# One run for the seven output products, 64x64 scan-input products in two banks, and new dates in the planner of an attention kernel

## The chip, the core and the metric

The kernel runs on one core of a Trainium2 chip. The metric is the device time of one execution in microseconds (us); the time of before is the median of three executions. The profile comes from one further execution. Engine names are those of the profile: PE is TensorE (matmuls), PEld its weight loads, DVE is VectorE, ACT is ScalarE, POOL is GpSimd, SP the queue that issues most DMAs.

## The reference, cut to what matters

One sequence of 4096 rows by 512, a context of 3202 rows, 8 heads of 64, all float32. Layer norm of both, multi-head cross attention with output weights `W_o`, residual; then a layer norm, a projection to 64 scan inputs, a scan over all 4096 rows, its states times `Cmat` added, and a constant row.

```python
x = residual + _mha(layernorm(x), layernorm(ctx), W_qkv, b_qkv, W_o, b_o)
residual = x
U = (layernorm(x) @ W_in.T + b_in) @ Bmat           # 4096 x 64
def step(s, u_t):
    s = jax.nn.silu(s @ A.T) + u_t
    return (s, s)
_, states = jax.lax.scan(step, zeros, U)
x = residual + states @ Cmat + mod
```

## The kernel before, in words

**Lead.** For the first 195 us keys and values are computed from the context and stored in DRAM. **Attention.** The 4096 query rows are eight blocks of 512 (`Q` 0 to 7). A block has 8 units (4 pairs of heads by 2 halves of 256 rows), and a unit has 13 steps over the keys. A step is a batch of scores (L1133, tile `s`, two PSUM buffers), an exponential on ACT (L1211, tile `p`, a ring of 11), a running sum of the exponentials on DVE (L1219, tile `acc`) and a batch of products with the values (L1269, tile `po`), four steps later. Scores and value products use the PE array as four 64x64 quarters: four matmuls run at once, one on each quarter. A full step is 8 matmuls of each kind, which the trace holds as 16 records, two for each float32 matmul. Two quarters that read different rows write to different PSUM banks. The sums over keys (`sums`, L1298, tile `pd`) and the first guess of the maximum (`sample`, `spread`, L1153 and L1175, tile `sm`) are also in quarters.

**Between the steps** stands the rest of a block, and it repeats from block to block. The query projection of the next block (`by_sevenths`) and the output projection of the last one (`project_by_sevenths`) are products of two 2x2 block matrices, done with seven block products instead of eight, with the whole 128x128 array (`seventh`, L393, 8 records for each of the seven). They accumulate in two PSUM banks, x and y, in the order 1, 2, 6, 5, 7, 3, 4 (`CHAIN`). After each product its bank is read (`read`), and the next product into the same bank waits for that read, so there is a chain PE, reader, PE with one other product between. The readers are ACT and DVE in turn for the queries, and DVE alone for the outputs (L1667, `outs.read`). Four sums of operands (`sum_`, L1649, pieces `so`) are made on DVE for products 5, 6, 7 and 3. In the output projection, sum 5 is made only after product 1 (`open_left` is called by product 1, and the plan says so), product 5 waits for it, and so the seven products are broken into three runs with scores between. In the query projection the sums are made ahead, and its seven products are one run.

After the output projection each half block of 256 rows goes through a second layer norm, is transposed (DVE `flip`, then DMAs `move0` to `move3` on SP into tile `xn2`), and is multiplied with the 512x64 matrix `wc` to give the scan inputs (`inputs`, L1729, tile `pu`): for each of 4 chunks and 2 row tiles one matmul of 128 rows by 64 columns, 16 records, all into one PSUM bank. ACT reads the bank with two activations (`kept_rows`, L1758) into the tile `u`.

**Ring m.** `sample`, `sums`, the seven products and `inputs` share two PSUM banks, the ring `m`; whoever takes them waits until the reader of the one before has given them back.

**Order.** All pieces of the attention part go through `Plan`: a piece has an engine, a cost, the pieces it needs, a due time, rings that it takes, and a `kind`. `order` walks through time and gives each free engine the ready piece that is due first. A due time is shifted for each sort of piece by the table `SHIFT` (in steps of 2150 ns). On PE, pieces of kind `"quarters"` and pieces without a kind are told apart: changing over costs `ENTER` or `LEAVE` in the plan, and a piece that would stand alone in the other mode is put off by `ALONE`. The order that comes out is the program's order on each engine; nothing is reordered on the chip between engines' queues. Scores, value products, `sums`, `sample` and `spread` are quarters; `inputs` and the seven products are not.

**Tail.** The last block has only its first half projected in this way (`project`); the last 256 rows follow at the end (`last_rows`): output product L2076, layer norm, transposes (L334, L2115), their scan inputs (L2125), and a short scan of 20 dependent steps (tile `zl` and, for the last four, `py_o`, L1924 with ACT L2161). Beside it runs the main scan's second sweep, 16 dependent steps (tile `z`, L1924, ACT L1952, DVE L1959), and the rows of the output (L1998, then ACT, POOL, DVE and a store).

Of the kernel before, what the change touches and what calls it, by code (L numbers as in the profile page):

```python
# [75 lines left out]
class Plan:  # L76
# [11 lines left out]
    KEEP, ALONE = 6000, 30000  # L88
# [5 lines left out]
        "row.store": -0.5, "fold": 17, "rows.outs": 10.5, "heads": -12, "spread": 1.75, "query.flip": -11,  # L94
        "states": -17, "inverse": 14.75, "extra": 10, "scale": -55.75, "rest": 11, "row.mod": -20,
        "joined0": -6.25, "b": -1, "add.l": -23, "l.stats": -34.25, "last": -4.5, "base": -34.75,
        "inverse.l": -35, "rows.inputs": 6, "maximum": -13.75, "fall": -19, "query.stats": -4, "den": 6.5,
        "row.scaled": 16, "l.h": -11, "row.stats": -21.25, "rows.turn": 13, "query.scaled": 7.5, "l.mod": 7.5,
        "close": -10, "swap": -2.25, "products": -9, "gather.l": -4, "l.ys": -10, "fall.l": -2.5,
        "weights": -3.5, "rows.s": 2, "l.x1": 1, "l.kept": 6, "tq": 20, "l.store": 10, "row.move3": 11,  # L100
        "l.from": -5, "l.copy": -12, "l.states": -8, "l.turn": 4, "row.flip": 3.75, "swap.l": -18, "l.near": 4,
        "differ": 12.25, "row.load": 12, "add": -6, "rest.l": -8, "den.l": 11.5, "query.factors": 16,
        "sevenths": -6, "l.z": 1, "scale.l": -0.5, "outs": -3, "output": -12, "query.move3": 3, "number": 0.25,
        "l.inputs": -4, "q": -12, "sums": -4, "row.move2": 2, "row.move1": -0.25, "query.move0": 1.5,
        "stored1": -12, "counted": 1, "to": 12, "sums.l": 1, "row.kept": 8, "so": 10.75, "stored0": 2,
        "l.scaled": -0.25, "row.move0": 4, "rise": 3, "join": -12, "sample": 3.5, "l.idle": 11.75,
        "risen": -0.5, "c2": 1, "yb": 2, "query.load": 8, "query.move2": -4, "row.row": -0.5, "added": -12,
        "l.terms": 13, "joined1": 2,
# [23 lines left out]
    def order(self):  # L132
# [11 lines left out]
        last, now, port, before, events, out = None, 0, 0, None, [], []  # L144
# [7 lines left out]
        def fits(p):  # L152
            if shares(p) and port + (self.LATE["DVE"] if gated(p) else 0) > now:
                return False
# [7 lines left out]
        while len(out) < len(pieces):  # L162
            for e in self.LATE:
# [22 lines left out]
                for r in p["take"]:  # L186
                    taken[r].append(p["name"])
# [2478 lines left out]
```

## Time and profile before

| | us |
|---|---|
| median of 3 executions | 1901.77 (1901.64 to 1901.78) |
| the profiled execution's own time | 1901.72 |
| its span in the profile | 1899.8 |
| PE busy | 1884.8 (99%) |
| DVE busy | 1545.2 (81%) |
| ACT busy | 1178.1 (62%) |
| POOL busy | 253.5 (13%) |

The profiled execution's own time is 1.9 us more than its span. A matmul's start in the trace is measured and its end is modelled, and matmuls overlap; so the time of a stretch of PE work is read from the start of its first matmul to the start of the first matmul behind it. From 351.4 us to 1594.2 us the trace repeats itself every 207.1 us, six times, once for each block; the seventh projection falls into the stretch behind it. The page's section on the chain that ended last is empty in this profile, so what bounds the kernel is read from stretches and from the order in time.

### The profile page before, as it was taken

What the parts mean: (1) busy time and instruction counts of PE and PEld (TensorE: products, weight loads), DVE (VectorE), ACT (ScalarE), POOL (GpSimd) and SP (SyncE); (2) the same over time, 40 slices, a digit from 0 to 9 for tenths busy, and PEclk for the clock granted to TensorE, in tenths of its full rate; (3) what the DMA queues carried; (4) which work ended last, traced back from release to release, by engine and by line L of the source; (5) the groups of instructions that cost most, each with busy time, mean ns of one, the idle gap of its engine ahead of it and who ended that gap; (6) DMA issues with size and microseconds to landing.
All of it is one profiled execution on the core that took longest, in us unless ns stands there. A gap on an engine that the chain in (4) does not pass through costs nothing.

```text
span 1899.8 us, 68757 instructions
## 1 busy us (share of the span) xinstructions
PE 1884.8 (99%) x29632; PEld 1383.5 (73%) x29632; DVE 1545.2 (81%) x2114; ACT 1178.1 (62%) x1677; POOL 253.5 (13%) x386
## 2 busy tenths in 40 slices
PE   9999999999999999999999999999999999999997
PEld 5887678777777777777777777777777777777684
DVE  6642699788978898799978897889969997988776
ACT  3242677575767567666766576657766675657653
POOL 6120300022000310022002200021002200120105
PEclk9999999999999999999999999999999999999999
DMA  8654233133323343223413332324312331536476
GB/s 254 159 158 118 59 103 91 41 112 91 97 74 105 92 110 89 77 76 105 112 43 113 83 110 78 105 78 113 101 55 89 112 104 44 171 111 177 136 200 225
DMA packets 260768, 207.55 MB, mean 109 GB/s; under 512 B 94632, under 2 KB 233896, under 8 KB 260460
## 3 DMA queue, kind: packets, MB, share of 16 engines
q1 hardware_dynamic: 256440, 196.48, 36.3%
q10 hardware_dynamic: 4020, 6.62, 1.2%
q8 instruction: 235, 3.85, 0.9%
q14 instruction: 73, 0.60, 0.1%
HBM read 156.32 MB, written 29.88 MB: 98 GB/s over the span
## 4 chain that ended last, share of the span: by engine, by line


## 5 line engine op out<-in xcount | busy, mean ns | idle before, releaser
L1211 ACT ACTIVATE p<-s,shifts 128x1024 f32<-128x1024 f32 (+1 forms) x832 | 895.0, 1082 | 458.1 <-PE s L1133 441.4
L1219 DVE TENSOR_TENSOR acc<-p,acc 128x1024 f32<-128x1024 f32 (+1 forms) x704 | 838.1, 1191 | 107.8 <-ACT p L1211 82.9
L1269 PE MATMUL po<-p,v 64*64 64x256 f32 x12800 | 849.5, 377 | 0.9 <-DVE o L1324 0.9
L1133 PE MATMUL s<-q,k 64*64 64x256 f32 x12800 | 850.1, 377 | 0.3 <-ACT p L1211 0.2
L1133 PEld LDWEIGHTS s<-q,k 64*64 64x64 f32 x12800 | 505.0, 133 | 197.2 <-ACT p L1211 12.9
L1269 PEld LDWEIGHTS po<-p,v 64*64 64x64 f32 x12800 | 504.0, 133 | 172.1 <-issue 6.9
L1622 POOL TENSOR_TENSOR xr<-xr,rowb 128x512 f32<-128x512 f32 x28 | 35.4, 1275 | 842.5 <-DVE acc L1219 842.5
L1347 DVE RECIPROCAL rd<-rd 128x256 f32<-128x256 f32 (+1 forms) x64 | 110.1, 1720 | 9.7 <-ACT rd L1342 9.7
L1219 DVE TENSOR_TENSOR acc<-p,p 128x1024 f32<-128x1024 f32 x64 | 78.1, 1220 | 26.5 <-ACT p L1211 26.4
L1713 POOL TENSOR_TENSOR xr<-x,modb 128x512 f32<-128x512 f32 x28 | 35.5, 1277 | 197.5 <-DVE acc L1219 155.5
L1243 DVE TENSOR_TENSOR acc<-swap,acc 64x256 f32<-64x256 f32 x126 | 56.1, 446 | 1.8 <-ACT swap L1238 0.2
L1204 DVE TENSOR_TENSOR acc<-x,acc 2x256 f32<-2x256 f32 x128 | 54.9, 429 | 1.4
L1409 POOL TENSOR_SCALAR rstd_x<-mv_x 128x1 f32<-128x1 f32 x28 | 18.9, 677 | 269.7 <-DVE mv_x L1406 268.0
L1559 ACT ACTIVATE q<-qx,bias 128x256 f32<-128x256 f32 x42 | 17.6, 471 | 56.8 <-PE qx L393 56.8
L1238 ACT COPY swap<-acc 64x256 f32<-64x256 f32 x126 | 50.9, 404 | 3.0
L571 DVE TENSOR_TENSOR ks<-pky,ks 128x512 f32<-128x512 f32 x15 | 10.4, 692 | 42.9 <-PE pky L393 28.1
L565 ACT ACTIVATE ks<-pkx,bias 128x256 f32<-128x256 f32 x40 | 16.8, 471 | 42.7 <-PE pkx L393 31.2
L1226 DVE TENSOR_TENSOR acc<-acc 128x512 f32<-128x512 f32 x63 | 42.9, 682 | 0.4
L1324 DVE TENSOR_TENSOR o<-po,o 128x256 f32<-128x256 f32 x64 | 26.9, 421 | 8.8 <-ACT o L1320 8.7
L1342 ACT ACTIVATE rd<-pd 128x128 f32<-128x128 f32 x126 | 33.6, 276 | 0.1
L1417 ACT ACTIVATE xh_y<-x,nm_y,rstd_y 128x512 f32<-128x512 f32 x30 | 24.3, 808 | 13.1 <-POOL nm_y L1411 13.1
L1167 DVE TENSOR_REDUCE m<-sm 128x1 f32<-128x256 f32 x64 | 23.8, 413 | 10.1 <-PE sm L1153 10.1
(312 smaller groups left out, 1754.2 us busy)
## 6 DMA issues: line engine op xcount, KB each, us to landing
k<-kd SPq DMA_DIRECT2D x432, 128.0 KB, 2.3
v<-vd SPq DMA_DIRECT2D x432, 128.0 KB, 2.3
xn<-x SPq DMA_DIRECT2D x448, 32.0 KB, 1.9
xr<-in_x_dram SPq DMA_DIRECT2D x30, 256.0 KB, 3.8
x1d<-xr SPq DMA_DIRECT2D x30, 256.0 KB, 2.8
x<-in_x_dram SPq DMA_DIRECT2D x28, 256.0 KB, 3.0
cx<-in_ctx_dram SPq DMA_DIRECT2D x25, 256.0 KB, 5.0
kd<-ks SPq DMA_DIRECT2D x20, 256.0 KB, 2.3
```

The costliest lines, as they stand in the source:

```text
L1133: nc.tensor.matmul(s[k0 : k0 + HD, a, b, :], kts[(*w["at"][:2], c)][r, b * CK + k0 : b * CK + k0 + HD], q[r], start=True, stop=True, skip_ ...
L1204: made = nc.vector.tensor_tensor(to[r], t[r], to[r], ALU.add)
L1211: nc.scalar.activation(t[:, :, :nb, :], w["ps"][c][:, :, :nb, :], AF.Exp, bias=w["shift"])
L1219: return nc.vector.tensor_tensor(w["acc"][:, :, :nb, :], t[:, :, :nb, :], before[:, :, :nb, :], ALU.add)
L1226: return nc.vector.tensor_tensor(acc[:, :, 0, :], acc[:, :, 0, :], acc[:, :, 1, :], ALU.add)
L1238: nc.scalar.copy(w["swap"][r], of[(1 - k) * HD : (2 - k) * HD])
L1243: made = nc.vector.tensor_tensor(of[r], w["swap"][r], of[r], ALU.add)
L1269: nc.tensor.matmul(w["po"][k][a * HD : (a + 1) * HD, :QU], vts[Q, hp, c][r, b, a * HD : (a + 1) * HD], t[r, a, b, :], start=(c == 0 and b ...
L1342: nc.scalar.activation(to, of, AF.Copy, accum_out=rises[:, 3 * i + k : 3 * i + k + 1])
L1347: nc.vector.reciprocal(w["rd"][:, part], (w["pd"] if last else w["rd"])[:, part])
L1622: return nc.gpsimd.tensor_tensor(xs[half][:, t], xs[half][:, t], rowb, ALU.add)
L1713: return nc.gpsimd.tensor_tensor(xt[:, t], x1[:, t], modb, ALU.add)
```

## The change

**Output projection.** The four operand sums of the output projection no longer wait for product 1 and product 5's sum no longer follows it; sum 5 opens the operands itself (`open_left` returns at once when they are open). Product 1 now waits for sums 6 and 7. Reads of both projections get a due time earlier by `ALONE`, which puts them ahead of other ready pieces of their engine. A new rule in `fits` keeps an engine from beginning a piece that would hold up an expected read by more than `WAITS` (600 ns).

**Scan inputs.** Each matmul of `inputs` is split by its 128 rows into two of 64, one for each of two banks, and the piece becomes a `"quarters"` piece that takes both banks of ring m: 16 matmuls (32 records) in place of 8 (16 records). ACT moves the first bank, with bias and scale, into the start of `xn2` (`first`, one 128x128 activation in place of two 64x128), and DVE adds the second bank to it and writes `u` (`kept_sums`, two SCALAR_TENSOR_TENSOR of 64x128). The tail's own inputs (L1843 and L2125) stay as they were.

**Dates.** The table `SHIFT` gets other numbers for nearly all sorts and 22 more sorts; the due times of almost all pieces of the attention part move.

```diff
-    KEEP, ALONE = 6000, 30000
+    KEEP, ALONE, WAITS = 6000, 30000, 600
+    CHAINS = "outs", "sevenths"
...
-        "row.store": -0.5, "fold": 17, "rows.outs": 10.5, "heads": -12, "spread": 1.75, "query.flip": -11,
+        "row.store": 2.25, "fold": 21, "rows.outs": -27.25, "heads": 29.5, "spread": 4.5, "query.flip": -21,
...
         def fits(p):
+            if any(now < r < now + p["cost"] - self.WAITS for r in reads.get(p["engine"], [])[-2:]):
+                return False
...
+                    if p["name"][0] in self.CHAINS:
+                        on = pieces[(p["name"][0] + ".read", *p["name"][1:])]["engine"]
+                        reads[on].append(now + cost + self.LATE[e])
...
         def open_left():
+            if left:
+                return
...
             if k == "5":
+                open_left()
...
-            after = {"5": scales(*a21) + scales(*a22) + [(*key, "1")], "6": [("so", Q, "5")],
+            after = {"5": scales(*a21) + scales(*a22), "6": [("so", Q, "5")],
...
-            "1": scales(*a11) + [("to", "4")] + [(*k, "row") for ks in kss for k in ks],
+            "1": scales(*a11) + [("to", "4")] + [("so", Q, k) for k in "67"]
+            + [(*k, "row") for ks in kss for k in ks],
...
-            plan.add(("outs.read", Q, k), "DVE", 690, partial(read, k), [(*key, k)], d + at,
+            plan.add(("outs.read", Q, k), "DVE", 690, partial(read, k), [(*key, k)], d + at - plan.ALONE,
...
-            w["pu"] = m_tile([P, P], f"pu_{at[0]}")
+            w["pu"] = [m_tile([P, P], f"pu_{at[0]}_{k}") for k in range(2)]
...
-                    nc.tensor.matmul(
-                        w["pu"][t * NS : (t + 1) * NS], wc[:, c, :], mixed(w["xn"][:, c, :], t),
-                        start=(c == 0), stop=(c == NC - 1), skip_group_check=True,
-                    )
+                    for k in range(2):
+                        r = slice(k * HD, (k + 1) * HD)
+                        nc.tensor.matmul(
+                            w["pu"][k][t * NS : (t + 1) * NS], wc[r, c, :], mixed(w["xn"][r, c, :], t),
+                            start=(c == 0), stop=(c == NC - 1), skip_group_check=True,
+                        )
...
-        plan.add((*k2, "inputs"), "PE", 850, inputs, copied + [from_(d + (gate + 12) * STEP)],
-                 d + 16 * STEP, ["m"], [("xn2", xn2)])
+        plan.add((*k2, "inputs"), "PE", 900, inputs, copied + [from_(d + (gate + 12) * STEP)],
+                 d + 16 * STEP, ["m", "m"], [], "quarters")
+
+        def first():
+            w["sum"] = w["xn"][:, 0, :P]
+            nc.scalar.activation(w["sum"], w["pu"][0], AF.Identity, bias=bu2, scale=2.0)
...
+    def kept_sums(w, at, t):
...
+        nc.vector.scalar_tensor_tensor(
+            u[hs, :, c0 : c0 + P // L].rearrange("s j c -> s c j"),
+            w["pu"][1][of].rearrange("s (c j) -> s c j", j=L),
+            2.0,
+            w["sum"][of].rearrange("s (c j) -> s c j", j=L),
+            ALU.mult,
+            ALU.add,
+        )
```

What this makes of the order, first on PE at the output projection of block 1. Names: `pax` and `pay` are the banks x and y, `s` scores, `po` value products; in the kernel before, the middle one of the three runs:

```order
L1133 MATMUL s_0_1_11_7775<-q_0_6561,k_0_0_11_7156 64x256 x8
L393 MATMUL pay_7735<-to_2260,so_7756 128x256 x4
L393 MATMUL pax_7734<-to_2260,so_7756 128x256 x4
L393 MATMUL pay_7735<-wo,o_2_0_6209 128x256 x4
L393 MATMUL pax_7734<-to_2316,o_0_1_5181 128x256 x4
L1269 MATMUL po_2_0_1_7585<-p_0_1_7_7664,v_0_0_7_7158 64x256
```

Ahead of this stand products 1 and 2, then a batch of `po` and one of `s`; behind it stand batches of `po`, `s` and `po`, and then product 4 alone. In the changed kernel, the same place on PE:

```order
L1280 MATMUL po_2_0_1_7599<-p_0_1_9_7749,v_0_0_9_7232 64x256
L404 MATMUL pax_7840<-wo,o_0_0_4720 128x256 x4
L404 MATMUL pay_7841<-wo,o_2_0_6211 128x256 x4
L404 MATMUL pax_7840<-to_2277,so_7785 128x256 x4
L404 MATMUL pay_7841<-to_2277,so_7785 128x256 x4
L404 MATMUL pax_7840<-to_2337,o_0_1_5177 128x256 x4
L404 MATMUL pay_7841<-wo,o_2_0_6211 128x256 x4
L404 MATMUL pax_7840<-to_2337,o_2_1_6583 128x256 x4
L1144 MATMUL s_1_0_1_7913<-q_0_6602,k_1_0_1_7561 64x256 x8
```

The seven are one run, and it begins about two steps later in the block than the first of the three runs did; this holds for all seven blocks that have it. On DVE, which reads the banks (L1667 before, L1682 after) and makes the sums (L1649 before, L1664 after), the same place in the kernel before:

```order
L1667 TENSOR_TENSOR x_512_7754<-pax_7734,xr_7182 128x2x256
L1649 TENSOR_TENSOR so_7756<-o_0_1_5181,o_2_1_6567 128x512
L1667 TENSOR_TENSOR x_512_7754<-pay_7735,x_512_7754 128x2x256
L1649 TENSOR_TENSOR so_7756<-so_7756,o_0_0_4721 128x512
L1649 TENSOR_TENSOR o_0_1_5181<-o_0_0_4721,o_0_1_5181 128x512
L1649 TENSOR_TENSOR o_2_0_6209<-o_2_0_6209,so_7756 128x512
L1219 TENSOR_TENSOR acc_0_1_7530<-p_0_1_8_7688,acc_0_1_7530 128x1024
L1667 TENSOR_TENSOR x_768_7798<-pay_7735,xr_7214 128x2x256
```

And on DVE in the changed kernel, from the read of product 1 to that of product 3:

```order
L1682 TENSOR_TENSOR x_512_7857<-pax_7840,xr_7200 128x2x256
L1230 TENSOR_TENSOR acc_0_1_7549<-p_0_1_10_7760,acc_0_1_7549 128x1024
L1682 TENSOR_TENSOR x_512_7857<-pay_7841,x_512_7857 128x2x256
L1664 TENSOR_TENSOR o_2_0_6211<-o_2_0_6211,so_7785 128x512
L1682 TENSOR_TENSOR x_512_7857<-pax_7840,xr_7200 128x2x256
L1230 TENSOR_TENSOR acc_0_1_7549<-p_0_1_11_7792,acc_0_1_7549 128x1024
L1682 TENSOR_TENSOR x_768_7884<-pay_7841,xr_7255 128x2x256
L1230 TENSOR_TENSOR acc_0_1_7549<-p_0_1_12_7812,acc_0_1_7549 128x2x256
L1237 TENSOR_TENSOR acc_0_1_7549<-acc_0_1_7549 128x2x256
L1682 TENSOR_TENSOR x_768_7884<-pax_7840,x_768_7884 128x2x256
L1682 TENSOR_TENSOR x_512_7857<-pay_7841,x_512_7857 128x2x256
```

Three of the four sums now stand ahead of the run, and between two reads stand at most two other pieces. In the tail, on PE behind the last output products, the kernel before has the second transpose, then two scan steps with rows of the output, then the second half's inputs (L2125), and the terms of the short scan (`zl`) behind the seventh step of the main scan:

```order
L1998 MATMUL pd_last<-c_21297,scan 64x256 x8
L1924 MATMUL z<-scan,a_t 64x128 x2
L2125 MATMUL py_o_24447<-xn_l,wc 64x128 x4
L1924 MATMUL z<-scan,a_t 64x128 x2
L1924 MATMUL z<-u,a_t 64x512 x2
...
L1924 MATMUL z<-scan,a_t 64x128 x2
L1924 MATMUL zl<-scan,a_t 64x128 x8
L1924 MATMUL py_o_24447<-scan,a_t 64x128 x2
```

In the changed kernel the inputs of both halves stand together behind the second transpose, and the terms of `zl` follow behind the third step of the main scan:

```order
L2151 MATMUL py_o_24587<-ident,xh_yl_24599 128x128 x4
L2161 MATMUL pu_l_24615<-xn_l,wc 64x128 x4
L2161 MATMUL py_o_24587<-xn_l,wc 64x128 x4
L1960 MATMUL z<-scan,a_t 64x128 x2
...
L1960 MATMUL zl<-scan,a_t 64x128 x8
L1960 MATMUL py_o_24587<-scan,a_t 64x128 x2
L1960 MATMUL z<-scan,a_t 64x128 x2
L2034 MATMUL pd_last<-c_21416,scan 64x256 x4
```

The short scan moved ahead by four steps of the main scan, which now stand behind its start. The lead, up to the first scores, stands on every engine as before.

More of the change, by code (lines that the diff above doesn't have):

```diff
@@ L99 @@
[L99 to L103, printed above, removed]
@@ L143, in order @@
         free = dict.fromkeys(self.LATE, 0)
-        last, now, port, before, events, out = None, 0, 0, None, [], []
+        last, now, port, before, reads, events, out = None, 0, 0, None, dict(DVE=[], ACT=[]), [], []
         def shares(p):
```

38 lines of the change are left out of this document (26 added, 12 removed).

## The prediction, made before the change was run

> **What bounds the kernel now.** I began with the busy shares, then cut the span into stretches, and then read PE's order in time at the places that the change touches.
>
> ```profile
> span 1899.8 us, 68757 instructions
> PE 1884.8 (99%) x29632; PEld 1383.5 (73%) x29632; DVE 1545.2 (81%) x2114; ACT 1178.1 (62%) x1677; POOL 253.5 (13%) x386
> ```
>
> The table by stretches has, behind each span, the busy time of PE, PEld, DVE, ACT and POOL; here are the first and the last of six equal periods, and the end:
>
> ```profile
> 351.40:558.50 207.10, 207.07 (x3541) 150.50 (x3541) 179.07 (x234) 137.24 (x188) 22.61 (x32) 1.00 0.33 91
> ...
> 1387.10:1594.20 207.10, 207.07 (x3544) 150.41 (x3540) 179.23 (x234) 137.39 (x189) 22.62 (x32) 1.00 0.32 91
> ...
> 1850.00:1899.80 49.80, 38.89 (x490) 24.03 (x490) 31.63 (x76) 15.61 (x53) 24.71 (x31) 0.94 0.71 227
> ```
>
> PE is occupied for 207.07 of 207.1 us, at the full clock (1.00), while DVE has 28 us and ACT 70 us free. So PE is the bound, and work moved to DVE is free as long as PE does not wait for it. But "busy" covers drains, so I go to the starts. The output projection of block 1, all of PE's rows:
>
> ```profile
> 635.59 1.24 PE L1269 MATMUL po<-p,v 64*64 64x256 f32 x16
> 636.46 1.24 PE L1133 MATMUL s<-q,k 64*64 64x256 f32 x16
> 637.62 1.99 PE L393 MATMUL pax<-wo,o 128*128 128x256 f32 x8
> 639.45 1.89 PE L393 MATMUL pay<-wo,o 128*128 128x256 f32 x8
> 641.27 1.09 PE L1269 MATMUL po<-p,v 64*64 64x256 f32 x16
> 642.19 1.04 PE L1133 MATMUL s<-q,k 64*64 64x256 f32 x16
> 643.16 1.99 PE L393 MATMUL pay<-to,so 128*128 128x256 f32 x8
> ...
> 648.44 1.89 PE L393 MATMUL pax<-to,o 128*128 128x256 f32 x8
> 650.26 1.09 PE L1269 MATMUL po<-p,v 64*64 64x256 f32 x16
> ...
> 651.61 1.04 PE L1269 MATMUL po<-p,v 64*64 64x256 f32 x16
> 652.58 1.99 PE L393 MATMUL pax<-to,o 128*128 128x256 f32 x8
> 654.51 1.09 PE L1133 MATMUL s<-q,k 64*64 64x256 f32 x16
> ```
>
> A batch of 16 quarter records takes 0.87 us (635.59 to 636.46). Each time PE leaves the quarters it loses more: 636.46 + 0.87 is 637.33 and the first product starts at 637.62 (0.29 lost), 643.06 against 643.16 (0.10), 652.48 against 652.58 (0.10). The runs themselves last 3.65, 7.10 and 1.93 us up to the next quarter matmul, 12.68 together.
>
> **Term 1, one run in place of three.** What one run costs is in the trace, since the query projection has the same seven products with the same shapes:
>
> ```profile
> 752.70 0.61 PE L1269 MATMUL po<-p,v 64*64 64x256 f32 x8
> 753.24 1.99 PE L393 MATMUL qx<-xn,wq 128*128 128x256 f32 x8
> ...
> 763.70 1.89 PE L393 MATMUL qx<-xn,wq 128*128 128x256 f32 x8
> 765.52 1.09 PE L1133 MATMUL s<-q,k 64*64 64x256 f32 x16
> ```
>
> It lasts 12.28 us, with 0.11 at its entry (8 records are 0.43): 12.39. Now the outputs cost 12.68 + 0.29 + 0.10 + 0.10 = 13.17. The difference is 0.78 us a block. Of it 0.19 is the surplus of the first entry (0.29 against 0.10), which no row explains and which may stay; I count **0.59**, and keep 0 to 0.19 more for the range. Seven blocks: 4.1 us.
>
> **Term 2, scan inputs in quarters.** The two places in one block:
>
> ```profile
> 690.94 1.04 PE L1133 MATMUL s<-q,k 64*64 64x256 f32 x16
> 691.92 1.09 PE L1729 MATMUL pu<-xn,wc 128*64 128x128 f32 x16
> 692.94 1.09 PE L1269 MATMUL po<-p,v 64*64 64x256 f32 x16
> ...
> 735.87 1.15 PE L1269 MATMUL po<-p,v 64*64 64x256 f32 x16
> 736.94 1.09 PE L1729 MATMUL pu<-xn,wc 128*64 128x128 f32 x16
> 737.97 1.09 PE L1133 MATMUL s<-q,k 64*64 64x256 f32 x16
> ```
>
> The first costs 0.11 at the entry (690.94 + 0.87 to 691.92) and 1.02 up to the next batch, the second 0.20 and 1.03: 2.36 us a block. The new form, 32 records of 64x64 by 128 columns, does not occur, but `pd` has records of that very shape in the same mode:
>
> ```profile
> 655.42 0.40 PE L1298 MATMUL pd<-acc,ones 64*64 64x128 f32 x8
> 655.64 1.04 PE L1269 MATMUL po<-p,v 64*64 64x256 f32 x16
> ```
>
> 8 records in 0.22 us, so 32 in 0.88 and two places in 1.76. Gain 0.60 us a block, seven blocks: 4.2 us. Its bounds are no loss of mode changes at all (0.60) and, should the doubled count cost as much as the changes saved, 0.
>
> **What DVE and ACT get.** For each half block ACT gives up two activations and takes one, and DVE takes two additions. Prices:
>
> ```profile
> L1758 ACT ACTIVATE u<-pu,bu 64x128 f32<-64x128 f32 x30 | 14.4, 480 | 5.9 <-PE pu L1729 4.9 <-PE pu L1843 0.7
> L1952 ACT ACTIVATE scan<-z 128x128 f32<-128x128 f32 x16 | 4.5, 279 | 14.7 <-PE z L1924 14.7
> L1959 DVE SCALAR_TENSOR_TENSOR scan<-scan,z 128x128 f32<-128x128 f32 x16 | 4.5, 284 | 7.6 <-ACT scan L1952 5.9 <-PE zl L1924 1.6
> ```
>
> ACT: 2 x 0.48 less, 0.28 more, so 1.4 us a block less. DVE: four additions a block at 0.28, or 0.48 if writing `u` with its stride costs DVE what it costs ACT: 1.1 to 1.9 us of the 28 that are free. That hides, on average. What doesn't follow from an average is the place: both banks of ring m are now held until DVE has added, and in the new order `sums` stands three batches behind the first half's inputs, 3 x 0.87 = 2.6 us. From the last input to the freed banks it takes one activation and two additions, 0.28 + 0.56, behind at most one running exponential and one running `acc` (1.1 and 1.2 us, row below). That is 0.8 to 3.2 us, so at worst 0.6 us of waiting; DVE's order has a row statistic and no `acc` just ahead of the additions, so I count nothing.
>
> **The wait that the change makes tight** is the read of each product. Rows of DVE:
>
> ```profile
> 645.26 0.69 DVE L1667 TENSOR_TENSOR x<-pay,xr 128x512 f32<-128x512 f32 x1 [0.18 <-PE pay L393]
> 645.87 1.22 DVE L1219 TENSOR_TENSOR acc<-p,acc 128x1024 f32<-128x1024 f32 x1
> 647.00 0.68 DVE L1667 TENSOR_TENSOR x<-pax,xr 128x512 f32<-128x512 f32 x1
> ```
>
> Product 5 starts at 643.16 and is read from 645.26 on: 2.1 us after its start. A product comes every 1.73 us ((648.44 - 643.16 - 0.10) / 3, the 0.10 being what a run loses behind its first matmul), and the product that needs this read starts 3.46 + 0.10 after it. Left over: 3.56 - 2.10 - 0.69 = 0.77 us. In the new order I followed DVE's queue with these rows (a read holds the next piece up for 0.61 us, an `acc` for 1.13): the reads of products 1, 2, 6, 5 and 7 end at 2.8, 4.5, 6.2, 8.0 and 9.8 us of the run, and the products that need them start at 3.6, 5.3, 7.0, 8.7 and 10.5. Every one fits, the least margin is 0.7 us. Scores wait 12.4 us in one piece now instead of 7.1; ACT idles there, but its 70 free us cover that.
>
> **Dates and tail.** The lead is unchanged, and the six periods stay alike in the new order, so what goes wrong in one does so seven times. DMA pieces are moved, not added. In the tail the order changes most:
>
> ```profile
> 1864.78 0.36 DVE L2132 TENSOR_SCALAR scan<-py_o,bu 64x128 f32<-64x128 f32 x1
> 1868.64 1.04 PE L1924 MATMUL zl<-scan,a_t 64*64 64x128 f32 x16
> 1884.08 0.38 PE L1924 MATMUL z<-scan,a_t 64*64 64x128 f32 x4
> 1889.77 0.28 PE L1924 MATMUL py_o<-scan,c 64*64 64x32 f32 x4
> 1892.32 0.66 PE L2218 MATMUL py_a<-c,scan 64*128 64x512 f32 x1 [1.18 <-DVE scan L2171]
> ```
>
> The inputs of the short scan are ready at 1865.14 and its terms start 3.5 us later, in line behind the main scan; its last step (1889.77) then leads to the last rows. In the new order the terms stand four main steps earlier, so up to 3.5 us come off. Against it, the main scan's last step (1884.08) is pushed back by what now goes ahead of it: the terms (1.04 us) and perhaps two short steps of (1889.77 - 1868.64) / 20 = 1.06 us, 3 us in all, and its rows may then end last. Both ends are as near to the rows, and of the two scans the short one ends last now: I take **-1.0**, from -3.5 to +3.
>
> **The sum.** From the profiled execution's own 1901.7 us: 4.1 + 4.2 + 1.0 = 9.3 less, **1892.4 us**; the median of before is the same 1901.8. Own range: 1888.6 with all of 0.19 x 7 and 3.5 in the tail, 1896.4 with the tail at +3.
>
> **Rivals.**
>
> 1. *The reads come late.* The price of one read behind a whole `acc` is 1.22 - 0.77 = 0.45 us, at five products of a run: 2.2 us a block, 15.7 in all, 1892.4 + 15.7 = **1908.1, slower**. It decides from 1.3 us of waiting in a run, where a block's 1.19 us of gain and the tail are used up. Against it speak the margins above; for it, that now all five reads are made and waited for within a run, and before two were, in the middle one.
> 2. *The small matmuls are bound by their number, not by their columns.* If a record goes on costing what a record of `pu` costs now (1.02 / 16 = 64 ns), 32 take 2.04 us and not 0.88: 1.16 more at 14 places, 16.2 us, so **1908.6, slower**. The 0.22 us for 8 records of `pd` (27 ns each) speak against it, though 8 are fewer than 32. The Trainium skill, TensorE: Matmul & The Clock Gate, section "Wait — 56ns, not 53.3ns?", gives about 62 ns of sequencer time per matmul when the decoding in hardware is off, as the bound of small ones; by that rule the change would lose about as much. The trace, with 27 ns a record, does not agree for runs of 8.
> 3. *The gain is taken back elsewhere in the block*: at the banks of ring m (0.6 us), at the scores behind the longer run, at a sum that DVE makes late; 0.6 to 1.2 us a block, 4.2 to 8.4 us: **1896.6 to 1900.8**, about no change. The Trainium skill, TensorEngine Tiling (Array Packing), section "PSUM Bottleneck", warns that tiling speeds up the matmuls and not the reading of PSUM, and the change does lengthen that reading; no row here shows it as a limit.
> 4. *The change does not do what it says*: ruled out for the order, which shows one run and quarters.
>
> **Chances.** Forecast 0.75, rival 1 0.09, rival 2 0.04, rival 3 0.12. A measurement of this kernel can tell about 0.2%, 3.8 us, from no change, so faster is below 1898.0 and slower above 1905.6. Faster holds the forecast and a third of rival 3: 0.79; same the rest of rival 3: 0.08; slower is rivals 1 and 2: 0.13. The range reaches from 1888.6 to 1899.0, with the forecast's own range and half of rival 3: it leaves out 2 in 10.
>
> **What would show it.** A period of 205.9 us in place of 207.1. One run of `pax` and `pay` in a block, some 12.3 us from its first start to the next scores, with 1.73 us from product to product; a longer distance there, released by DVE L1682, is rival 1. The inputs as 32 records in 0.9 us between two batches, with no gap: 2 us would be rival 2. No wait of `pd` behind them. The terms of `zl` some 4 us sooner after their inputs. I would be wrong if the period stayed at 207, or if the tail from the first `za` on became longer by more than 3 us.

## The result and the profile after

The changed kernel takes **1889.12 us** (median of 6 executions, 1888.87 to 1889.67) beside 1901.72 us for the kernel before (6 executions, 1901.18 to 1902.16): a ratio of 0.9934, 95% interval 0.9921 to 0.9947, or 12.6 us less. The forecast was 1892.4, in a range from 1888.6 to 1899.0. The profiled execution of after has a time of its own of 1889.67 us, that of before 1901.72: 12.05 less. Of these 11.95 lie within the span (1899.84 and 1887.89 us), and that is what the rows below have to add up to.

The page's busy shares, and one of the equal periods in the table by stretches (columns as before: PE, PEld, DVE, ACT, POOL, granted clock, DMA share, GB/s):

```profile
span 1887.9 us, 69209 instructions
PE 1873.1 (99%) x29856; PEld 1414.9 (75%) x29856; DVE 1563.3 (83%) x2142; ACT 1166.6 (62%) x1663; POOL 258.2 (14%) x386
```

```profile
556.75:762.10 205.35, 205.35 (x3570) 152.46 (x3569) 181.42 (x238) 135.62 (x186) 23.27 (x32) 1.00 0.32 92
```

PE is still the bound, occupied for the whole of a period at the full clock; DVE and ACT still have 24 and 70 us free. The period itself is read from one query projection to the next. Before (its start at 753.24 us stands in the prediction) and after:

```profile
960.32 1.99 PE L393 MATMUL qx<-xn,wq 128*128 128x256 f32 x8
```

```profile
751.83 1.99 PE L404 MATMUL qx<-xn,wq 128*128 128x256 f32 x8
957.22 1.99 PE L404 MATMUL qx<-xn,wq 128*128 128x256 f32 x8
```

960.32 - 753.24 is 207.08; 957.22 - 751.83 is 205.39, and the other five periods of after are 205.32 or 205.33. A period gives **1.75 us**, where the prediction's two terms gave 1.19.

The output projection of block 1, which was three runs, is one:

```profile
640.33 1.04 PE L1280 MATMUL po<-p,v 64*64 64x256 f32 x16
641.30 1.99 PE L404 MATMUL pax<-wo,o 128*128 128x256 f32 x8
...
651.77 1.89 PE L404 MATMUL pax<-to,o 128*128 128x256 f32 x8
653.59 1.09 PE L1144 MATMUL s<-q,k 64*64 64x256 f32 x16
654.50 1.04 PE L1280 MATMUL po<-p,v 64*64 64x256 f32 x16
```

12.29 us from 641.30 to 653.59, 1.73 us from product to product ((651.77 - 641.30 - 0.10) / 6), 0.11 lost at the entry (640.33 + 0.86 to 641.30). One more loss shows here that the prediction left out: the batch behind the run takes 0.91 (653.59 to 654.50) and not 0.86.

The scan inputs at their two places in the block:

```profile
695.64 1.04 PE L1280 MATMUL po<-p,v 64*64 64x256 f32 x16
696.50 1.19 PE L1747 MATMUL pu<-xn,wc 64*64 64x128 f32 x29
697.42 0.38 PE L1144 MATMUL s<-q,k 64*64 64x256 f32 x1
697.51 0.28 PE L1747 MATMUL pu<-xn,wc 64*64 64x128 f32 x3
697.62 1.04 PE L1144 MATMUL s<-q,k 64*64 64x256 f32 x15
```

```profile
733.14 1.04 PE L1280 MATMUL po<-p,v 64*64 64x256 f32 x16
734.00 1.05 PE L1747 MATMUL pu<-xn,wc 64*64 64x128 f32 x32
734.88 1.04 PE L1144 MATMUL s<-q,k 64*64 64x256 f32 x16
735.74 0.61 PE L1280 MATMUL po<-p,v 64*64 64x256 f32 x8
```

At the second place 32 records take 0.88 us with nothing lost on either side, as forecast. The first place looks different: one record of scores stands among the last records of `pu`. One quarter of the array has gone ahead of the other three. This broken group, "x29, x1, x3" where "x32" is meant, turned out to be the sign to look for, and the kernel before has it too, at a place that the prediction passed over.

**What stands behind the attention part.** PE's first row behind the last value product is at 1846.97 us before and at 1835.85 after:

```profile
1846.97 1.98 PE L2076 MATMUL yb<-wo,o 128*128 128x512 f32 x4
```

```profile
1835.85 1.08 PE L1296 MATMUL pd_last<-acc,ones 128*64 128x256 f32 x8
```

From there PE has the same work in both kernels. Up to there 11.1 us are gained, 10.5 of them in the six periods, and from there to the end of the span 0.8 us more.

### The profile page after: what moved, and what is told of

Read it like the earlier page. It is cut to its first block, busy times and chain, and to the rows that moved or that the text cites. A ratio compares the mean times of both kernels' runs of the same rounds, so it can differ in the third digit from the quotient of the medians.

```text
span 1887.9 us, 69209 instructions
## 1 busy us (share of the span) xinstructions
PE 1873.1 (99%) x29856; PEld 1414.9 (75%) x29856; DVE 1563.3 (83%) x2142; ACT 1166.6 (62%) x1663; POOL 258.2 (14%) x386
## 4 chain that ended last, share of the span: by engine, by line
PE 97%; DVE 1%; ACT 1%; DMA 0%; issue 0%; POOL 0%; SPq 0%; DVEq 0%; ACTq 0%; POOLq 0%
PE po L1280 37%; PE s L1144 36%; PE pax L404 3%; PE qx L404 3%; PE qy L404 2%; PE pay L404 2%; PE pkx L404 2%; PE pvx L404 2%; PE pvy L404 1%; PE pky L404 1%; PE pk L722 1%; PE pv L599 1%; PE pd L1309 1%; PE sm L1164 1%; PE po L1268 1%; PE pu L1747 1%
## 5 line engine op out<-in xcount | busy, mean ns | idle before, releaser
L1230 DVE TENSOR_TENSOR acc<-p,acc 128x1024 f32<-128x1024 f32 (+1 forms) x704 | 851.0, 1214 | 96.8 <-ACT p L1222 77.2
L1144 PEld LDWEIGHTS s<-q,k 64*64 64x64 f32 x12800 | 518.9, 133 | 175.2 <-ACT p L1222 13.5
L1280 PEld LDWEIGHTS po<-p,v 64*64 64x64 f32 x12800 | 519.9, 133 | 163.1 <-issue 3.5
L1729 POOL TENSOR_TENSOR xr<-x,modb 128x512 f32<-128x512 f32 x28 | 41.6, 1496 | 253.3 <-DVE acc L1254 178.3
L481 DVE STREAM_TRANSPOSE x<-xh_y 128x512 f32<-128x512 f32 x28 | 18.2, 688 | 21.7 <-ACT xh_y L1428 14.7
```

Source lines behind the costliest of these rows:

```text
L1144: nc.tensor.matmul(s[k0 : k0 + HD, a, b, :], kts[(*w["at"][:2], c)][r, b * CK + k0 : b * CK + k0 + HD], q[r], start=True, stop=True, skip_ ...
L1230: return nc.vector.tensor_tensor(w["acc"][:, :, :nb, :], t[:, :, :nb, :], before[:, :, :nb, :], ALU.add)
L1280: nc.tensor.matmul(w["po"][k][a * HD : (a + 1) * HD, :QU], vts[Q, hp, c][r, b, a * HD : (a + 1) * HD], t[r, a, b, :], start=(c == 0 and b ...
L1729: return nc.gpsimd.tensor_tensor(xt[:, t], x1[:, t], modb, ALU.add)
```

## The experiments

The theory at the start: PE is the bound, so the gain is a sum of times that PE lost and no longer loses: at changes of mode (outputs, inputs), and in a wait ahead of `sums` that the new dates take away. The rival: the new dates make a better order as a whole, and the two code changes carry little. In the table the period is the distance between the starts of two query projections that most of the six distances show (in outs_only, inputs_only, old_dates and old_dates_sums one or two are 0.1 to 0.4 us longer), and the ratio is to the kernel before, run on the same chip beside it (1901.5 us).

| kernel | dates | outputs | inputs | us | ratio, 95% | period |
|---|---|---|---|---|---|---|
| before | old | 3 runs | 16 records | 1901.5 | | 207.08 |
| outs_only | old | 1 run | 16 records | 1897.64 | 0.9977 (0.9967 to 0.9987) | 206.26 |
| inputs_only | old | 3 runs | quarters | 1902.44 | 1.0005 (0.9996 to 1.0014) | 206.93 |
| old_dates | old | 1 run | quarters | 1892.54 | 0.9951 (0.9937 to 0.9965) | 205.78 |
| new_dates | new | 3 runs | 16 records | 1901.52 | 1.0000 (0.9991 to 1.0009) | 206.54 |
| outs_new_dates | new | 1 run | 16 records | 1894.47 | 0.9962 (0.9948 to 0.9975) | 205.72 |
| after | new | 1 run | quarters | 1889.12 | 0.9934 (0.9921 to 0.9947) | 205.33 |
| full_rows | as after, matmuls of 128 rows | | | 1892.45 | 0.9951 (0.9937 to 0.9964) | 205.71 |
| sums_later | before, one `sums` moved | | | 1898.08 | 0.9980 (0.9971 to 0.9989) | 206.47 |
| old_dates_sums | old_dates, one `sums` moved | | | 1888.68 | 0.9932 (0.9918 to 0.9947) | 205.16 |
| inputs_later | after, one `inputs` moved | | | 1891.51 | 0.9948 (0.9934 to 0.9961) | 205.30 |
| reads_late | after, three reads moved | | | 1892.79 | 0.9954 (0.9940 to 0.9967) | 205.84 |
| twice | after, inputs issued twice | | | 1900.88 | 0.9998 (0.9988 to 1.0007) | 207.07 |

### The parts one by one

**new_dates**: the kernel before with the table of after, nothing else.

```diff
-        "row.store": -0.5, "fold": 17, "rows.outs": 10.5, "heads": -12, "spread": 1.75, "query.flip": -11,
+        "row.store": 2.25, "fold": 21, "rows.outs": -27.25, "heads": 29.5, "spread": 4.5, "query.flip": -21,
...
```

> The kernel before with nothing but the new table of dates: output products still in three runs, scan inputs still as 16 records of 128 rows. Theory A (the gain is the sum of PE's lost times, and the two code changes carry it: 0.92 us a block at the outputs, 0.69 at the inputs, 0.43 at a wait in front of `sums` that the new dates take away, 0.28 given back elsewhere): 0.15 to 0.43 us a block, so 1 to 3 us faster than before, 1899 to 1901, the period 206.7 to 206.9. Theory B (the order that the new dates make is what gains): 5 us faster or more, below 1897.

The time is that of before. The period is 0.54 us shorter, more than expected, but from the last value product on this kernel takes 2.1 us longer than before (the last `po` record starts at 1844.20 of a span of 1899.5, before at 1846.66 of 1899.84). So the dates by themselves are worth nothing here: what they gain in the blocks they lose in the tail. Of the 2.1 us there 0.5 lie ahead of DVE's last read (L2221 in the kernel before) and 1.7 behind it, with the last stores; why the stores take longer in this kernel is not known.

**outs_new_dates**: after with the scan inputs of before.

```diff
-            w["pu"] = [m_tile([P, P], f"pu_{at[0]}_{k}") for k in range(2)]
+            w["pu"] = m_tile([P, P], f"pu_{at[0]}")
...
-        plan.add((*k2, "inputs"), "PE", 900, inputs, copied + [from_(d + (gate + 12) * STEP)],
-                 d + 16 * STEP, ["m", "m"], [], "quarters")
+        plan.add((*k2, "inputs"), "PE", 850, inputs, copied + [from_(d + (gate + 12) * STEP)],
+                 d + 16 * STEP, ["m"], [("xn2", xn2)])
...
```

> The changed kernel with the old scan inputs (16 records, one bank, two activations), so new dates and one run of output products. Theory A: the changed kernel's 1889.1 plus 7 x 0.69 for the inputs, 1893.9, and a period of 206.0; below the run with the new dates alone by 7 x 0.92 = 6.4. Theory B: within 1.5 us of the run with the new dates alone.

The one run of outputs gives 0.82 us a period (206.54 to 205.72), the inputs 0.39 (to 205.33). The rival falls: the code changes carry 1.2 of the 1.75.

**full_rows**: after in its own order, only the matmuls of the scan inputs on the full 128 rows.

```diff
-                    for k in range(2):
-                        r = slice(k * HD, (k + 1) * HD)
-                        nc.tensor.matmul(
-                            w["pu"][k][t * NS : (t + 1) * NS], wc[r, c, :], mixed(w["xn"][r, c, :], t),
+                    nc.tensor.matmul(
+                        w["pu"][0][t * NS : (t + 1) * NS], wc[:, c, :], mixed(w["xn"][:, c, :], t),
...
-        w["pu"][1][of].rearrange("s (c j) -> s c j", j=L),
-        2.0,
+        w["pu"][0][of].rearrange("s (c j) -> s c j", j=L),
+        0.0,
```

> The changed kernel, order and all, but each scan-input matmul on the full 128 rows (16 records of 128x64 into the first bank; the addition on VectorE reads that bank with the factor 0, so its work is the same and the sums come out right). Theory A: 0.69 us a block more for the change of mode at entry and exit and 64 in place of 54 ns a record: period 206.0, 1893.9. If only the place in the order of the new quarters piece gained, it is as fast as the changed kernel: 1889.1. If small matmuls were bound by their number, it would be faster than the changed kernel.

The form of the matmuls alone is worth 0.38 us a period, not 0.69. Its second place, to be held against the four rows of after above:

```profile
733.53 1.04 PE L1280 MATMUL po<-p,v 64*64 64x256 f32 x16
734.51 1.09 PE L1745 MATMUL pu<-xn,wc 128*64 128x128 f32 x16
...
736.45 0.83 PE L1280 MATMUL po<-p,v 64*64 64x256 f32 x12
```

From `po` to `po` it takes 2.92 us here and 2.60 in after (735.74 - 733.14): 0.32 gained. So the first place can have gained only 0.07. Why is in the rows of ACT in after:

```profile
695.81 0.83 ACT L1206 ACTIVATE x<-sm,shifts 128x256 f32<-128x256 f32 x2
```

These two activations (the piece `extra`) read the two banks of ring m that `sample` and `spread` wrote. They end at 696.64. The inputs now take both banks: the first matmul in line, on one quarter, writes the first bank and starts at 696.50; the second needs the second bank, and the other three quarters start at 696.70, 0.19 late. The old inputs took one bank, the one read first, and did not wait.

**old_dates**: after with the table of before.

> Both code changes with the table of dates of before. Theory A: the outputs (one run in six of seven blocks, 5 and 2 in the last) and the inputs gain as in the changed kernel, the wait in front of `sums` may stay: 0 to 0.43 us a block slower than the changed kernel, 1889 to 1893 with the tail within 1 us. Theory B: less than half of the gain, above 1895.

9.0 us faster than before, out of 12.4. The new table adds 3.4 us to the two code changes (0.45 us a period), though it gave nothing without them. Two parts of the answer to "where" come from the runs with one code change each.

**outs_only** and **inputs_only**: before with the old dates and one of the two code changes.

> The kernel before with the old dates and old scan inputs, and only the output projection changed: sums made ahead, seven products in one run (in the last block 5 and 2), reads first in line. Prediction's term 1: 0.59 us a block, period 206.49, 4 us faster, 1897.5, and the surplus of 0.19 at the entry stays, since the wait of `sums` ahead of it stays. With what a run also loses in the batch behind it (0.05 for each of two runs saved): 0.70 a block, period 206.4. Rival (the 0.82 a block that the run costs less under the new dates is the code's own): period 206.26.

> The kernel before with the old dates and the old output projection, and only the scan inputs changed to quarters in two banks. Prediction's term 2: 0.60 us a block, period 206.48, 4.2 us faster, 1897.3, if both places find the two banks of ring m free. Rival (the form gains only 0.39 a block, as between two of the kernels with the new dates): period 206.69, 1898.8.

The outputs give 0.82 us a period, as under the new dates: that gain belongs to the code. (What the earlier reads and the new rule in `fits` give within it was not run alone; reads_late below prices the reads.) The inputs alone give 0.15, and their kernel is not faster as a whole. The reason is an order that came about with the changed piece: at the second place three batches of scores follow each other with no value products between, and the third waits for its PSUM buffer until an exponential has read it.

```profile
729.93 1.04 PE L1133 MATMUL s<-q,k 64*64 64x256 f32 x15
731.28 1.09 PE L1133 MATMUL s<-q,k 64*64 64x256 f32 x16 [0.30 <-ACT p L1211]
...
733.06 1.05 PE L1731 MATMUL pu<-xn,wc 64*64 64x128 f32 x32
```

729.93 + 0.86 is 730.79, the next batch starts at 731.28: 0.49 us lost just ahead of inputs that are themselves whole (x32).

### One wait, moved by one place

What did the kernel before lose that the new dates took away? Its rows around the one `sums` that comes soon after a `spread`; the columns are start, duration, engine, line, operation, tiles and number of records:

```profile
628.91 1.04 PE L1133 MATMUL s<-q,k 64*64 64x256 f32 x16
629.98 0.70 PE L1298 MATMUL pd<-acc,ones 64*64 64x128 f32 x5
630.36 0.43 PE L1269 MATMUL po<-p,v 64*64 64x256 f32 x1
630.50 0.28 PE L1298 MATMUL pd<-acc,ones 64*64 64x128 f32 x3
...
631.28 1.24 PE L1133 MATMUL s<-q,k 64*64 64x256 f32 x16
```

```profile
629.46 0.83 ACT L1195 ACTIVATE x<-sm,shifts 128x256 f32<-128x256 f32 x2
```

```profile
629.01 0.86 DVE L1243 TENSOR_TENSOR acc<-swap,acc 64x256 f32<-64x256 f32 x2
```

The same sign: "x5, x1, x3" and batches that last 1.24 in place of 1.04. `sums` needs both banks of ring m, and `extra` reads the second until 630.29. One quarter starts at 629.98, the others at 630.34, 0.05 us behind the end of `extra`. (The sum over keys on DVE, which `sums` needs too, is done at 629.87.) Up to the next scores the leading quarter loses 631.28 - 628.91 - 0.86 - 0.22 - 0.86 = 0.43 us. The other three are 0.19 behind it, batch after batch, and pay when the quarters have to meet: at the first output product, the 0.29 at the entry that the prediction could not explain.

**sums_later**: before, with this one `sums` of each block behind the next batch of value products.

```diff
-        for piece in plan.order():
+        pieces = plan.order()
+        for Q in range(1, NQB):
+            at = [p["name"] for p in pieces].index(("sums", 8 * Q - 1))
+            behind = next(i for i in range(at, len(pieces)) if pieces[i]["name"][0] == "product")
+            pieces.insert(behind, pieces.pop(at))
+        for piece in pieces:
```

> The kernel before, with its old dates, where in each block one `sums` (that of the last unit of the block before) is moved by one place, behind the next batch of value products, and nothing else. Theory A (the dates' gain is this one wait: two banks of ring m are still being read by the two ScalarE activations of `extra`, L1195, when `sums` comes; the first quarter goes ahead, the others wait, 0.43 us at once and 0.19 more at the next 128x128 product, where the quarters meet again): the wait goes, period 207.08 - 0.62 = 206.46, the whole 7 x 0.62 = 4.3 us faster, 1897.2, and the 0.29 at the entry of the first output run becomes 0.10. Rival (the wait is for the sum over keys on VectorE, or the gain of the new dates lies in many small places): less than 0.2 us a block, above 1900.

```profile
629.92 0.40 PE L1298 MATMUL pd<-acc,ones 64*64 64x128 f32 x8
...
635.32 1.04 PE L1133 MATMUL s<-q,k 64*64 64x256 f32 x16
636.29 0.92 PE L393 MATMUL pax<-wo,o 128*128 128x256 f32 x3
```

The group is whole again (x8), the entry of the outputs costs 0.11 (635.32 + 0.86 to 636.29), and the period is 206.47: 0.61 us less, as worked out. So one place was the cause and not many small ones. Moving `sums` would have cured a wait for the sum on DVE as well, but the rows above rule that out for the three quarters: DVE was done 0.47 us before they started. The whole gains 3.4 and not 4.3 us, since the last block, outside the periods, gives some back.

**old_dates_sums**: the same move in old_dates.

> Both code changes with the old dates, and in each block the one `sums` moved by one place behind the next batch of value products. If the gains add up (period 205.78 with both code changes and old dates, 0.62 for the one wait): period 205.16, 7 x 0.62 = 4.3 us faster than the 1892.5 without the move, 1888.2, a little faster than the changed kernel with its new dates (1889.1). If the next wait takes the place of the one removed, as with the scan inputs moved later: 205.3 to 205.8, 1889 to 1892.

0.62 a period again, and 1888.68 us in all. That is as fast as after with its whole new table; the two can't be told apart by their intervals.

**inputs_later**: after, with the first inputs of each block behind the next batch of scores, and their readers directly behind them in line.

```diff
+            moved = ("rows", Q, 0, "inputs"), ("rows", Q, 0, "first"), ("row", Q, 0, "kept"), ("row", Q, 1, "kept")
+            at = [p["name"] for p in pieces].index(moved[0])
+            behind = next(p["name"] for p in pieces[at:] if p["name"][0] == "scores")
...
+            pieces[at:at] = [ours[name] for name in moved]
```

> The changed kernel with the first half block's scan inputs moved behind the next batch of scores, and their reader on ScalarE and two additions on VectorE directly behind them in line, ahead of one row statistic; nothing else moves. Theory A (the quarters' inputs lose 0.19 us at this place, because they now need both banks of ring m and the second is read until 0.19 us after the first record; the gain of the form itself is 0.58 us a block): period 205.33 - 0.19 = 205.14, 1.3 us faster than the changed kernel, 1887.8. Rival (the inputs' gain is only 0.39 by their form, or the wait moves to `sums` behind them): the period stays at 205.3.

The wait is gone, but the period shrinks by 0.03 only. PE is now 0.19 us earlier, and nine microseconds on it meets the next reader:

```profile
697.00 1.05 PE L1747 MATMUL pu<-xn,wc 64*64 64x128 f32 x32
...
706.09 2.09 PE L1280 MATMUL po<-p,v 64*64 64x256 f32 x32
707.82 1.23 PE L1144 MATMUL s<-q,k 64*64 64x256 f32 x16
```

```profile
705.75 0.42 DVE L1335 TENSOR_TENSOR o<-po,o 128x256 f32<-128x256 f32 x1
```

The first value products of a unit (706.09) need the two `po` banks of the unit before, and DVE reads the second behind an `acc`, until 706.17: three quarters start at 706.23 and later, and the batches last 1.23 from there. This kernel is 2.4 us slower than after as a whole: near the end PE stands still for 1.7 us ahead of `po` records at 1830.42, and for what is not known. So the wait of 0.19 is real, but in this order it is worth nothing to remove it alone.

### Two prices

**reads_late**: after, with the reads of products 1, 6 and 5 behind the running sum that follows them in DVE's line.

```diff
+            for k in "165":
+                at = [p["name"] for p in pieces].index(("outs.read", Q, k))
+                behind = next(i for i in range(at + 1, len(pieces)) if pieces[i]["engine"] == "DVE")
+                if pieces[behind]["name"][0] != "add":
+                    continue
+                pieces.insert(behind, pieces.pop(at))
```

> The changed kernel where in each block the reads of products 1, 6 and 5 on VectorE stand behind the running sum `acc` that now follows them; nothing else moves. By the rows of the changed kernel: the read of product 1 ends at 645.0 in place of 644.1 and product 6 wants it at 644.9, 0.2 us late; the other two still fit. So 7 x 0.2 = 1.4 us slower than the changed kernel, 1890.5. By the first rival's price of the prediction, 0.45 us for each read behind a whole `acc`: 7 x 1.35 = 9.5 us, 1898.6.

```profile
643.25 1.89 PE L404 MATMUL pay<-wo,o 128*128 128x256 f32 x8
645.39 1.99 PE L404 MATMUL pax<-to,so 128*128 128x256 f32 x8 [0.25 <-DVE x L1682]
647.22 1.89 PE L404 MATMUL pay<-to,so 128*128 128x256 f32 x8
```

```profile
642.18 2.55 DVE L1230 TENSOR_TENSOR acc<-p,acc 128x1024 f32<-128x1024 f32 x2
644.66 0.68 DVE L1682 TENSOR_TENSOR x<-pax,xr 128x512 f32<-128x512 f32 x1
```

0.51 us a period, between the two forecasts. Only the read of product 1 is late. It ends at 645.34; product 6, due at 643.25 + 1.73 = 644.98, starts at 645.39, 0.41 late, and then the run pays for its entry once more: 1.83 us to the next product and not 1.73. The order that puts the reads first is thus worth half a microsecond a block at this one product alone.

**twice**: after, with each scan-input matmul issued twice.

```diff
-            for c in range(NC):
+            for c in [*range(NC)] * 2:
```

> The changed kernel with every scan-input matmul issued twice, the second round of four chunks starting the sum anew, so the sums come out right: 64 records in place of 32 at each of 14 places. If a small record costs its columns (27 ns): 32 x 0.027 x 14 = 12.2 us more, 1901.3, the period 207.08. If small matmuls are bound by their number at 62 to 64 ns once there are more in a row: 2.0 us at each place, 28 us more, 1917.

```profile
736.16 1.93 PE L1747 MATMUL pu<-xn,wc 64*64 64x128 f32 x64
737.91 1.04 PE L1144 MATMUL s<-q,k 64*64 64x256 f32 x16
```

64 records in 1.75 us, 27 ns each, and the period is longer by 1.74, twice 32 x 0.027: they cost what their columns cost.

The Trainium skill, TensorE: Matmul & The Clock Gate, section "Wait — 56ns, not 53.3ns?", states about 62 ns for each matmul when decoding in hardware is off, and a floor of about 25 ns from start to start in either case. With 27 ns for each of 64 in a row the first does not hold in this run; the second is not put to the test, since four quarters run side by side and each starts a record every 109 ns (1.75 us / 16).

## Why the prediction was right, and where its sum was not

The time fell into the range, 3.3 us below the forecast, and the direction came from the terms that were forecast. Step by step:

- **PE is the bound**: so it is after (205.35 of 205.35 us in a period). But the reading of it was too coarse. A PE that is busy for 207.07 of 207.1 us still waited 0.6 us in each block, since records of the quarter that went ahead, and the modelled ends of the others, cover the gap.
- **Term 1, one run**: right in mechanism, too small. Forecast 0.59 us a block, measured 0.82 with old dates and with new. About 0.10 of the difference is the slower first batch behind each of the two exits saved (641.27 to 642.19 in the prediction's own rows is 0.92, where 0.87 was assumed). Most of the rest is at the second scan inputs, behind another broken group of `pd`: their entry costs 0.20 in before and in new_dates (734.90 + 0.87 to 735.97), and 0.11 once the outputs are one run, in outs_only (721.53 + 0.87 to 722.51) and outs_new_dates (733.37 + 0.86 to 734.34). The forecast had put this 0.09 into term 2. The surplus of 0.19 at the first entry was kept apart rightly: it does not belong to this part of the change.
- **Term 2, scan inputs in quarters**: forecast 0.60, measured 0.39 in after, and 0.48 under the old dates (206.26 to 205.78), where both places stand as one row of x32. Where the banks are free the form gains about what was said (0.32 at the second place, where 0.35 was forecast), but of other parts: without the 0.09 named above, and with 0.05 in the batch behind that the forecast left out. What failed is the step "ring m, I count nothing". I worked out how long the additions on DVE hold the two banks, for the `sums` behind, and there is no wait there. The wait is at the other end: taking two banks in place of one, the inputs themselves wait for `extra` on ACT, 0.19 us.
- **DVE and ACT get room**: right. The activation takes 0.37 us where 0.28 was said, an addition 0.37 on average between the 0.28 and 0.48 given (below), and DVE and ACT keep their 24 and 70 us.

```profile
L1782 DVE SCALAR_TENSOR_TENSOR u<-pu,xn 64x128 f32<-64x128 f32 x28 | 10.5, 374 | 3.1 <-ACT xn L1772 2.4
L1772 ACT ACTIVATE xn<-pu,bu 128x128 f32<-128x128 f32 x14 | 5.1, 367 | 7.1 <-PE pu L1747 6.5 <-ACT xh_y L1428 0.6
```

- **The reads fit**: right, with the margin that was given. The read of product 1 in after, which product 6 at 644.86 waits for, ends at 644.09, 0.77 us ahead:

```profile
643.40 0.69 DVE L1682 TENSOR_TENSOR x<-pax,xr 128x512 f32<-128x512 f32 x1
```

  Rival 1 was priced well for one read (0.45 forecast, 0.41 measured, and 0.10 for the new entry on top) but not for five: of three reads put behind an `acc`, two still fit.
- **Dates**: this step failed. "What goes wrong in one period does so seven times" was said, and then only the lead and the tail were looked at, and the dates counted as nothing. With both code changes they are worth 0.45 us a period and 3.4 us in all: a wait of 0.62 a block taken away (ahead of `sums`, with its echo at the outputs' entry) and one of 0.19 brought in (ahead of the first inputs, which in old_dates start whole, x32). Moving that one `sums` by hand gives the same. The row that told of it was quoted in the prediction: "0.29 lost" at the entry, "which no row explains". The rows eight microseconds earlier do.
- **Rivals**: rival 2 is ruled out by twice (27 ns a record), rival 4 by the rows. Rival 3, the gain taken back elsewhere in the block, had the better case than its 12% said: with the inputs changed alone it is what happened (0.49 of 0.6 us, inputs_only), and in after a third of the inputs' gain went the same way.
- **Tail**: forecast -1.0, measured -0.8 from the last value product on, but that the two agree is luck. The first half of the mechanism came as described. The short scan's first terms and last step, and the main scan's last step:

```profile
1851.19 1.04 PE L1960 MATMUL zl<-scan,a_t 64*64 64x128 f32 x16
1873.57 0.31 PE L1960 MATMUL py_o<-scan,c 64*64 64x32 f32 x4
1874.36 0.38 PE L1960 MATMUL z<-scan,a_t 64*64 64x128 f32 x3
```

  The inputs of the short scan are ready at 1851.02 and its terms start 0.2 us later (3.5 before). Counted from PE's first row behind the last value product, the short scan's last step comes 5.1 us sooner than before (37.7 against 42.8) and the main scan's last step 1.4 later (38.5 against 37.1), and what DVE has to do for the rows of the main scan and other small pieces now holds up the end: the short scan's last product is there at 1879.65 and is read at 1881.42 and 1883.29. The last row is the same read in before.

```profile
1881.42 0.68 DVE L2257 SCALAR_TENSOR_TENSOR xr_l<-py_a,xr_l 128x512 f32<-128x512 f32 x1
...
1883.29 0.68 DVE L2257 SCALAR_TENSOR_TENSOR xr_l<-py_o,xr_l 128x512 f32<-128x512 f32 x1
```

```profile
1894.27 0.68 DVE L2221 SCALAR_TENSOR_TENSOR xr_l<-py_o,xr_l 128x512 f32<-128x512 f32 x1
```

  Nothing is left of the five microseconds: this read comes 47.4 us behind PE's first row in after (1883.29 - 1835.85) and 47.3 in before (1894.27 - 1846.97). The 0.8 us lie behind it, with the last stores, from the read to the end of the span (4.6 us against 5.6). They do not hang on the order of the tail either: old_dates keeps the old one, its `zl` 3.5 us behind the inputs, and from the start of the last `po` record to the end it takes 52.34 us like after (53.17 in before). What sets the time from that read to the end, 4.6 to 7.2 us in these kernels, stays open.

**The sum.** The two code changes without the dates, old_dates, gain 9.0 us where 9.3 were forecast, in part by luck: term 1 was too small, term 2 too large, and 0.8 us came at the end for another reason than the one given. The step that failed is the one on the dates: 3.4 us counted as 0.

## What to carry to other kernels

Where an engine is busy for all of a period, read the distances between starts, batch by batch, against the same batch elsewhere; a group that should be one row and comes as "x5, x1, x3" shows that one quarter runs ahead of the others, and the wait that set them apart, which the busy share hides, stands there or further up. When a piece is changed to take more of a shared buffer, look at both ends: who waits for it afterwards, and whom it must now wait for. And an entry that costs more than its like is a bill from further up: go back to where the shift began before calling it unexplained.

## What the runs showed of the hardware

- The four 64x64 quarters of PE are not started together. When the next matmul in line has to wait for its bank, a quarter that has started goes on alone, and the others follow together: in before one starts `pd` at 629.98 and three at 630.34, and the first one's record of `po` starts at 630.36, behind the first `pd` records of the three and ahead of their second ones (630.50). So batches overlap, but at the two places shown here no matmul starts ahead of one that stands before it in the program: in after the third matmul of the inputs writes the first bank (L1745 to L1748), which the first matmul has already had, and still starts only with the second, at 696.70. The lead (0.19 us in before, over seven batches of 0.86) is kept until the full array or another wait brings the quarters together. The Trainium skill, TensorEngine Tiling (Array Packing), section "Key Properties", states that tiles operate independently and that a change of mode drains the engine, without a price for it. The trace agrees, and the price here is 0.11 at the entry, 0.10 behind the first full matmul, 0.09 at the exit and 0.05 in the batch behind it: 0.35 us for one way there and back.
- A wait inside a run of full matmuls costs its lateness and 0.10 us more for starting anew (reads_late).
- At a chain this tight a wait that is taken away can give way to the next one: 0.19 us gained ahead of the inputs came back as a wait for DVE nine microseconds later (inputs_later), and 0.49 of the 0.60 forecast for the quarters' form went at scores (inputs_only). It need not: the 0.62 ahead of `sums` came out whole (sums_later, old_dates_sums).
